# First loads in order of need, and the second feed-forward product by halves of its inner rows

## The chip, the cores and the metric

The kernel runs on one core of a Trainium2 chip. The metric is device microseconds of one execution. The median of three runs of the kernel before is 3042.24 us (3039.03 to 3044.84). The profiled execution, from which the tables below are taken, spans 3047.2 us.

## The reference

Two graph layers are applied to x (64 graphs, 256 nodes, 256 features), with an adjacency matrix of small integers for each graph; all is float32.

```python
# layer 0: two graph attentions, then a feed-forward
def gat(h, W, a):
    Wh = h @ W
    e = leaky_relu(Wh @ a[:256] + (Wh @ a[256:]).T, 0.2)
    att = softmax(where(adj > 0, e, -9e15), axis=1)
    return att @ Wh
h = layernorm(x + gat(gat(x, W1, a1), W2, a2))
x = layernorm(h + relu(h @ w_ff1 + b_ff1) @ w_ff2 + b_ff2)
# layer 1: attention with 8 heads, values by kind of edge, then a feed-forward
s = softmax(q @ k.T / sqrt(32))
o = sum over r in 0..3 of (s * (adj == r)) @ (x @ Wv[r])
x = layernorm(x + o @ Wo + bo)
x = layernorm(x + gelu(x @ W1 + b1) @ W2 + b2)
```

The inner width of both feed-forwards is 1024.

## The kernel before, in words

**Pairs of graphs.** The 64 graphs are handled as 32 pairs, each of which goes the whole way (`whole_way`, L943): the two graph attentions (`gat_layers`, L515), the first feed-forward (`feed_forward` with stage 0), the attention with heads (`attention`, L724), the second feed-forward (stage 2), and the store. Up to four pairs are under way at once. Since the adjacency takes only the values 0 and 1, two kinds of edge are enough; checks of the inputs' range are gathered on the way, and another program (`any_inputs`) would run if they failed.

**An order written out by a planner.** Each way is a Python generator. A step of it that needs TensorE yields the events it waits for, the names of locks it takes (such as "ff"), the number of PSUM banks that it needs, and, in further places, the buffers it needs. Work for the other engines is put into lists with `put` (L158), with a price in us, a rank, what it frees and what it needs. `run` (L213) is a list scheduler: it keeps a clock for each engine, starting at the values in `START` (L29), takes what can begin first, and emits the instructions in that order; `keep_order` then fixes this order on each engine. Loads that are emitted ahead of the planner have an assumed time of arrival: `landed` (L878) for groups of weights and the number given to `load` (L280) for the first two pairs. The planner only assumes them: at run time an instruction waits for its own data, and everything behind it in its engine's queue waits too. Among TensorE steps that could begin at once, the planner prefers those that are neither part of `reliefs` (the one-off preparation of biases) nor hold the lock "ff", so that feed-forwards fill what others leave.

**First loads.** SyncE issues them in the order of the program: the weights for W1 and W2 of layer 0, then the first pair's xT (transposed features), adjT (transposed adjacency) and x; the layernorm vectors; the feed-forward weights; the second pair's three; and then the weights of layer 1. The second pair's xT goes into the one buffer "input", which the first pair's xT holds until its last product of L528. VectorE adds bias vectors together at L899 once they are there, and L901 forms differences of weights.

**Feed-forward.** The first product (256 to 1024) is done with seven block products in place of eight (`Blocks`, L372): p1 to p7 with additions between them. There are two such sets, `slabs(0)` and `slabs(2)`, called a and b, of four of the eight inner blocks of 128 rows each: a has the inner blocks 0, 1, 4, 5 and b has 2, 3, 6, 7. Their results are held in four tiles named ff, two for each set. A chain runs through each set: a product in PSUM is copied by ScalarE (L687), VectorE adds further products to it (L392), and ScalarE applies bias and function (L693). The second product (1024 to 256, L712) has 32 matmuls: for graph b, for half j of its rows, over all eight inner blocks. It uses one PSUM bank for each graph b, and after the last matmul of a graph its layernorm begins. The last step of set b, `b.p3`, is put behind the first four matmuls. The lock "ff" is held from the first block product to the end of the second product.

**Transposing.** Between stages, features are transposed by VectorE in blocks and then by a round trip through DRAM; in five places at the start and the end of the kernel (`hurried`, L604) TensorE does it instead (L649), since then there is little other work to hide the round trip.

**Lines.** L528, L544, L557: the three products of a pair's graph attentions. L464: TensorE spreads a row of factors (first two pairs). L499 and L501: the attention weights on VectorE. L509: their scaling on ScalarE. L303 and L307: the adjacency made into bytes on ScalarE, and its largest values on VectorE. L681: block products of the first product of a feed-forward. L712: second product. L754, L759: queries, keys and values. L796: scores. L825, L828: attention times values, and sums. L847: output projection. L570: addition of the residual. L582 to L598: layernorm. L912, L921: one-off bias products. In the changed kernel these lines stand 6 to 12 further down.

Of the kernel before, what the change touches and what calls it, by code (L numbers as in the profile page):

```python
# [18 lines left out]
P = 128  # L19
# [8 lines left out]
SLACK = 0.3  # L28
START = {"tensor": 8.5, "vector": 8.0, "scalar": 4.0, "gpsimd": 0.0, "sync": 32.0}  # L29


@with_exitstack
def two_layers(ctx: ExitStack, tc: tile.TileContext, t: dict, out: bass.AP, flag: bass.AP):
# [95 lines left out]
    for m in range(KC):  # L129
# [11 lines left out]
    alone = {}  # L141
    free = {name: [0.0] * n for name, n in (("bank", 8), ("a", 2 * HQ), ("m", 2 * HQ), ("h", 2 * HQ), ("yb", 1), ("yT", 2), ("yTa", 1),
                                             ("input", 1), ("rows", 1), ("e", 2), ("adj", 4), ("sums_yT", 1), ("sums_yTa", 1), ("x", 4))}
# [69 lines left out]
    def run(besides, ways, together):  # L213
# [5 lines left out]
        while True:  # L219
# [8 lines left out]
            for n, (way, events, name, banks, *more) in enumerate(going):  # L228
                if all(alone.get(n) in (None, way) for n in name or ()) and all(e.time is not None for e in events):
                    at = begins(max([e.time for e in events], default=0.0), "bank" if banks else None, banks)  # L230
                    for needs in more:
                        at = None if at is None else begins(at, needs)
                    if at is not None:
                        times.append((at, n))
# [8 lines left out]
            if engine == "tensor":  # L243
                sure = [n for at, n in times if at <= now - SLACK]
                g = going[min(sure, key=lambda n: (going[n][0] is besides, "ff" in (going[n][2] or ()) or alone.get("ff") is going[n][0], n))
                          if sure else min(times)[1]]
                alone.update((name, g[0]) for name in g[2] or ())
                takes("bank", g[3])
                for needs in g[4:]:
                    takes(needs)  # L250
                step = next(g[0], None)
# [26 lines left out]


    def load(pair, at=None):  # L280

# [11 lines left out]
        def xT():  # L293
            to["xT"] = io.tile([P, KC, 512], F32, name="input")
            nc.sync.dma_start(to["xT"], t["xT"][pair].rearrange("(c p) b n -> p c (b n)", p=P))
# [24 lines left out]
        takes("x")  # L320
        for emit in (xT, adjT, x):
            emit()
        return to, [at_time(at), in_bytes(at_time(at)), at_time(at)]

# [47 lines left out]
    class Blocks:  # L372
# [24 lines left out]
        def p1(self):  # L397
            yield *self.first, 1
            self.begin()
            self.u1 = self.copy(0, 0, self.product(1, "x", 0, True))  # L400
# [114 lines left out]
    def gat_layers(pair, to, loads):  # L515
# [8 lines left out]
        for b in range(2):  # L524
# [6 lines left out]
            if b == 0:  # L531
                yield [], None, 2
        frees_at(clock["tensor"], ["input"] * (pair > 0))
        at_home, ratio, there = yield from addends(y, there, D + 2, 0, pair)
# [123 lines left out]
    def feed_forward(y, normal, w, func, relieved, gb, pair, stage):  # L658
# [11 lines left out]
        def slabs(t):  # L670
# [25 lines left out]

            first = ([normal[0], normal[1], relieved, second.there[0]], ["ff"]) if t == 0 else ([], None)
            blocks = Blocks(second, first, begin, multiply, target, copy, lambda of, event: activate(1, 0, event, of), activate)
# [3 lines left out]
        for step in (a.p1, b.p1, a.p2, a.p6, b.p2, b.p6, a.p5, a.p7, b.p7, b.p5, a.p4, b.p4, a.p3):  # L702
            yield from step()
        order, end = (0, 1, 4, 5, 2, 3, 6, 7), b.p3
        for b in range(2):
            for j in range(2):
                for part in (order[:half], order[half:]):
                    yield [evacuated[j][m] for m in part] if b == 0 else [], None, j == 0 and part[0] == 0
                    if j == 0 and part[0] == 0:
                        p2 = bank()  # L710
                    for m in part:
                        nc.tensor.matmul(p2[:, j * D:(j + 1) * D], lhsT=f[m][:, (2 * j + b) * P:(2 * j + b + 1) * P],  # L712
                                         rhs=w2[:, m, :], start=m == 0, stop=m == NF - 1)
# [686 lines left out]
```

## Time and profile before

| | |
|---|---|
| median of three runs | 3042.24 us |
| span of the profiled execution | 3047.2 us |
| TensorE matmuls (PE) | 2996.3 us busy, 19146 instructions |
| weight loads (PEld) | 2452.5 us busy |
| VectorE (DVE) | 2556.8 us busy |
| ScalarE (ACT) | 1752.5 us busy |
| GpSimd (POOL) | 252.6 us busy |
| second products of the two feed-forwards (L712) | 470.9 and 456.1 us busy |
| ScalarE loads of function tables | 70, of 1.28 us |
| transfers | 205.76 MB, mean 68 GB/s |

A float32 matmul appears as two instructions. Matmuls overlap, so the mean of one (about 380 ns) is longer than the pace at which they follow each other: eight instructions of L712 take 1.73 us. Busy time of an engine therefore says only when it has something to do. The places where TensorE has nothing to do are found in the idle time before its instructions, with the instruction whose end released it.

### The profile page before, as it was taken

The page shows a single profiled execution, that of the slowest core. Times are in us where ns is not written, and L with a number is a line of the kernel's source. Part 1 is how long each engine was busy: PE and PEld are TensorE (multiplying, and loading weights), DVE is VectorE, ACT ScalarE, POOL GpSimd, SP SyncE. Part 2 cuts the span into 40 slices and gives each one's busy share as a digit, 9 for nine tenths or more (in the row PEclk, how much of TensorE's full clock was granted, in tenths as well). Part 3 has the DMA queues.
Part 4 walks back from the last instruction along what each step waited for, and adds up shares of the span by engine and source line. Part 5 has one row for each costly group of instructions (what it writes and reads, how often), then busy time and mean ns, then how long its engine had stood idle before and what let it go on. Part 6 is the DMA issues. An engine that isn't in the chain of part 4 may idle for free.

```text
span 3047.2 us, 52870 instructions
## 1 busy us (share of the span) xinstructions
PE 2996.3 (98%) x19146; PEld 2452.5 (80%) x19146; DVE 2556.8 (84%) x5993; ACT 1752.5 (58%) x4096; POOL 252.6 (8%) x518
## 2 busy tenths in 40 slices
PE   7999999999999999999999999999999999999998
PEld 6887788878888888888888888888888888788876
DVE  5888988788988888888889888889888898888875
ACT  4556666556556556555565565565555655555654
POOL 0100010001100001100001000011000011000100
PEclk8999999999999999999999999999999999999999
DMA  5211041212212222112222112221122221122100
GB/s 186 74 47 61 32 127 54 70 56 84 70 40 66 77 84 77 53 53 70 84 84 77 39 60 77 84 77 62 50 68 79 84 77 52 52 71 70 49 1 22
DMA packets 211147, 205.76 MB, mean 68 GB/s; under 512 B 22336, under 2 KB 170432, under 8 KB 210880
## 3 DMA queue, kind: packets, MB, share of 16 engines
q1 hardware_dynamic: 210464, 202.06, 20.6%
q8 instruction: 153, 2.51, 0.4%
q14 instruction: 114, 0.93, 0.1%
q10 hardware_dynamic: 416, 0.26, 0.0%
HBM read 137.51 MB, written 64.73 MB: 66 GB/s over the span
## 4 chain that ended last, share of the span: by engine, by line
PE 63%; DVE 25%; DMA 6%; ACT 2%; SPq 1%; issue 1%; POOL 0%; DVEq 0%; ACTq 0%; POOLq 0%
PE ps L712 21%; PE ps L681 15%; PE ps L825 5%; DVE x L598 4%; PE ps L759 4%; PE ps L754 4%; PE ps L544 3%; DVE h L837 3%; PE ps L796 3%; DMA home<-yb 3%; DVE st L582 2%; DVE m L807 2%; PE ps L557 2%; DMA rows<-row 2%; DVE ff L392 2%; PE ps L847 2%
## 5 line engine op out<-in xcount | busy, mean ns | idle before, releaser
L712 PE MATMUL ps<-w_L_gnn_w_ff,ff 128*128 128x256 f32 x2048 | 470.9, 381 | 0.0
L712 PE MATMUL ps<-w_L_gnn_W,ff 128*128 128x256 f32 x2048 | 456.1, 380 | 1.8 <-ACT ff L693 1.8
L593 ACT ACTIVATE x<-x,less,rstd 128x256 f32<-128x256 f32 x512 | 279.2, 596 | 294.8 <-POOL less L589 294.7
L712 PEld LDWEIGHTS ps<-w_L_gnn_w_ff,ff 128*128 128x128 f32 x2048 | 386.6, 190 | 61.5 <-issue 9.8
L712 PEld LDWEIGHTS ps<-w_L_gnn_W,ff 128*128 128x128 f32 x2048 | 388.2, 190 | 57.6 <-ACT ff L693 2.6
L588 POOL TENSOR_TENSOR rstd<-rstd,mhalf 128x2 f32<-128x2 f32 x256 | 198.3, 775 | 2765.7 <-DVE less L585 2638.0
L807 DVE TENSOR_TENSOR m<-a,adj 128x512 f32<-128x512 f32 x512 | 350.1, 684 | 57.9 <-ACT a L803 57.8
L803 ACT ACTIVATE a<-ps 128x512 f32<-128x512 f32 x512 | 268.0, 604 | 222.6 <-PE ps L796 222.5
L681 PE MATMUL ps<-yT,w_L_gnn_W1p 128*128 128x256 f32 x1280 | 315.2, 382 | 4.7 <-ACT ff L687 2.4
L392 DVE TENSOR_TENSOR ff<-ps,ff 128x512 f32<-128x512 f32 x384 | 262.7, 685 | 66.4 <-PE ps L681 58.3
L681 PE MATMUL ps<-yT,w_L_gnn_w_ff1p 128*128 128x256 f32 x1280 | 308.8, 382 | 6.8 <-ACT ff L687 5.9
L681 PEld LDWEIGHTS ps<-yT,w_L_gnn_w_ff1p 128*128 128x128 f32 x1280 | 240.6, 190 | 50.8 <-ACT ff L687 18.8
L687 ACT ACTIVATE ff<-ps 128x512 f32<-128x512 f32 x384 | 223.9, 590 | 98.4 <-PE ps L681 97.6
L681 PEld LDWEIGHTS ps<-yT,w_L_gnn_W1p 128*128 128x128 f32 x1280 | 240.2, 190 | 48.2 <-ACT ps L835 8.5
L837 DVE RECIPROCAL h<-ps 128x256 f32<-128x256 f32 x128 | 223.4, 1746 | 21.3 <-PE ps L828 20.9
L509 ACT ACTIVATE xw<-xw,rs 128x258 f32<-128x258 f32 (+1 forms) x256 | 115.9, 502 | 200.7 <-DVE rs L504 200.6
L693 ACT ACTIVATE ff<-ff,c_L_gnn_b_ff 128x256 f32<-128x256 f32 x384 | 171.6, 504 | 97.4 <-DVE ff L392 97.0
L693 ACT ACTIVATE ff<-ff,c_L_gnn_b 128x256 f32<-128x256 f32 x384 | 173.3, 501 | 85.0 <-DVE ff L392 83.8
L811 DVE TENSOR_TENSOR h<-a 128x256 f32<-128x256 f32 x512 | 213.9, 418 | 0.0
L582 DVE BATCH_NORM_STATS2 st<-x 128x6 f32<-128x256 f32 x512 | 206.0, 402 | 0.9
L570 DVE TENSOR_TENSOR x<-ps,x 128x512 f32<-128x512 f32 x256 | 170.2, 682 | 16.4 <-PE ps L712 9.3
L769 ACT ACTIVATE qk<-ps,bqk 128x256 f32<-128x256 f32 x256 | 106.6, 468 | 112.2 <-PE ps L754 111.9
(128 smaller groups left out, 5008.1 us busy)
## 6 DMA issues: line engine op xcount, KB each, us to landing
home<-yb SPq DMA_DIRECT2D x182, 256.0 KB, 2.0
yT<-home SPq DMA_DIRECT2D x728, 64.0 KB, 2.0
rows<-row SPq DMA_DIRECT2D x60, 512.0 KB, 4.0
input<-in_xT SPq DMA_DIRECT2D x32, 512.0 KB, 5.1
x<-in_x SPq DMA_DIRECT2D x32, 512.0 KB, 3.8
out<-x SPq DMA_DIRECT2D x32, 512.0 KB, 5.1
input<-in_adjT SPq DMA_DIRECT2D x30, 512.0 KB, 4.5
v<-in_adjT SPq DMA_DIRECT2D x2, 512.0 KB, 7.3
```

The lines of the kernel that those rows point to most:

```text
L392: nc.vector.tensor_tensor(self.target(c, h), self.bank[bank], self.target(c, h), ALU.add)
L582: nc.vector.bn_stats(st[:, j, :], rows[j])
L588: nc.gpsimd.tensor_tensor(rstd, rstd, mhalf[:, :2], ALU.pow)
L593: nc.scalar.activation(rows[j], rows[j], AF.Identity, bias=less[:, j:j + 1], scale=rstd[:, j:j + 1])
L681: nc.tensor.matmul(to, lhsT=w1[:, a, (t + slab) * P:(t + slab + 1) * P], rhs=b, **flags)
L687: return put("scalar", 0.5, lambda: nc.scalar.activation(target(c, h), blocks.bank["x"], AF.Copy), event, rank=-1)
L693: evacuated[h][m] = put("scalar", 0.4, lambda m=m, to=to, source=source: nc.scalar.activation(to, source, func, bias=b1[:, m:m + 1]), even ...
L712: nc.tensor.matmul(p2[:, j * D:(j + 1) * D], lhsT=f[m][:, (2 * j + b) * P:(2 * j + b + 1) * P], rhs=w2[:, m, :], start=m == 0, stop=m == N ...
L803: nc.scalar.activation(a[n][o], ps[o], AF.Exp)
L807: nc.vector.tensor_tensor(m[n][o], a[n][o], adj, ALU.mult)
L811: nc.vector.tensor_tensor(h[n][o], a[n][o][:, :N], a[n][o][:, N:], ALU.add)
L837: there = put("vector", 1.68, lambda: nc.vector.reciprocal(s, po[:, N:]), there, rank=0)
```

## The change

The first part changes the order of the first loads: the second pair's xT and adjT are issued ahead of the feed-forward weights, x of each pair later than before, and the second pair's xT goes into the tile qk, which is not in use at that time, so that its load needn't wait for the first pair's. The times that the planner assumes for arrivals and for the engines' starts are set anew.

The second part splits the second product of a feed-forward by its inner rows: first all that the rows of set a contribute, for both graphs and both halves; then all of set b. Both graphs' PSUM banks are thus held throughout. After the first half the two ff tiles of set a are free. The lock "ff" is released when the second product has begun; a new lock "second" covers the rest of it. A first product now asks for two free ff tiles for each set. So the first product of another feed-forward can begin beside the second half of this one. A bank's start flag is set only by its first matmul. Steps that hold "second" have the same low preference as those with "ff".

```diff
-START = {"tensor": 8.5, "vector": 8.0, "scalar": 4.0, "gpsimd": 0.0, "sync": 32.0}
+START = {"tensor": 11.5, "vector": 11.5, "scalar": 4.0, "gpsimd": 0.0, "sync": 36.0}
...
-                g = going[min(sure, key=lambda n: (going[n][0] is besides, "ff" in (going[n][2] or ()) or alone.get("ff") is going[n][0], n))
+                g = going[min(sure, key=lambda n: (going[n][0] is besides, going[n][2] in (["ff"], ["second"]) or going[n][0] in (alone.get("ff"), alone.get("second")), n))
...
         def xT():
-            to["xT"] = io.tile([P, KC, 512], F32, name="input")
+            if at is not None and pair == 1:
+                to["xT"] = work.tile([P, 2, KC, 512], F32, name="qk")[:, 0]
+            else:
+                to["xT"] = io.tile([P, KC, 512], F32, name="input")
...
-        for emit in (xT, adjT, x):
+        for emit in (xT, adjT):
             emit()
-        return to, [at_time(at), in_bytes(at_time(at)), at_time(at)]
+        rest.append(x)
+        return to, [at_time(at[0]), in_bytes(at_time(at[1])), at_time(at[2])]
...
-            first = ([normal[0], normal[1], relieved, second.there[0]], ["ff"]) if t == 0 else ([], None)
+            first = ([normal[0], normal[1], relieved, second.there[0]], ["ff"], ("ff", 2)) if t == 0 else ([], None, ("ff", 2))
...
-        order, end = (0, 1, 4, 5, 2, 3, 6, 7), b.p3
-        for b in range(2):
-            for j in range(2):
-                for part in (order[:half], order[half:]):
-                    yield [evacuated[j][m] for m in part] if b == 0 else [], None, j == 0 and part[0] == 0
-                    if j == 0 and part[0] == 0:
-                        p2 = bank()
+        end, p2 = b.p3, {}
+        for first, part in ((True, (0, 1, 4, 5)), (False, (2, 3, 6, 7))):
+            for b in range(2):
+                for j in range(2):
+                    yield ([evacuated[j][m] for m in part] if b == 0 else []), ["second"] if first and b == j == 0 else None, first and j == 0
+                    if first and j == 0:
+                        p2[b] = bank()
                     for m in part:
-                        nc.tensor.matmul(p2[:, j * D:(j + 1) * D], lhsT=f[m][:, (2 * j + b) * P:(2 * j + b + 1) * P],
-                                         rhs=w2[:, m, :], start=m == 0, stop=m == NF - 1)
+                        nc.tensor.matmul(p2[b][:, j * D:(j + 1) * D], lhsT=f[m][:, (2 * j + b) * P:(2 * j + b + 1) * P],
+                                         rhs=w2[:, m, :], start=first and j == 0 and m == 0, stop=not first and m == NF - 1,
+                                         skip_group_check=True)
                     there = took(0.43 * len(part))
-                    if b == j == 0 and part[0] == 0:
+                    if first and b == 0 and j == 0:
                         yield from end()
                         frees_at(clock["tensor"], ["yT", "sums_yT"])
-            normal[b] = layernorm(y, gb, b, add_rows(y, p2, b, there), *([biased[1]] if onwards else []))
-            if onwards:
-                transposed(y, normal[b], normal, b, pair, 1)
-        done_with("ff")
+                        done_with("ff")
+                if not first:
+                    normal[b] = layernorm(y, gb, b, add_rows(y, p2[b], b, there), *([biased[1]] if onwards else []))
+                    if onwards:
+                        transposed(y, normal[b], normal, b, pair, 1)
+            frees_at(clock["tensor"], ["ff"] * 2)
+        done_with("second")
...
-    landed = {name: at_time(us) for name, us in (("ln0", 8.0), ("ff0", 15.0), ("attention", 30.0), ("ff1", 37.0))}
-    loaded = {0: load(0, 6.5)}
+    landed = {name: at_time(us) for name, us in (("ln0", 13.0), ("ff0", 23.0), ("attention", 35.0), ("ff1", 41.0))}
+    loaded = {0: load(0, (8.0, 9.5, 16.0))}
     ln = [layernorm_weights("L0_gnn_g_ln1", "L0_gnn_b_ln1", "L0_gnn_b_ff2")]
+    loaded[1] = load(1, (14.0, 15.5, 25.0))
+    rest[0]()
     ff0 = (first_weights("L0_gnn_w_ff1p"), column("L0_gnn_b_ff1"), weights("L0_gnn_w_ff2"))
-    loaded[1] = load(1, 18.0)
+    rest[1]()
```

More of the change, by code (lines that the diff above doesn't have):

```diff
@@ L141, in two_layers @@
     alone = {}
-    free = {name: [0.0] * n for name, n in (("bank", 8), ("a", 2 * HQ), ("m", 2 * HQ), ("h", 2 * HQ), ("yb", 1), ("yT", 2), ("yTa", 1),
+    free = {name: [0.0] * n for name, n in (("bank", 8), ("a", 2 * HQ), ("m", 2 * HQ), ("h", 2 * HQ), ("yb", 1), ("ff", NF // 2), ("yT", 2), ("yTa", 1),
                                              ("input", 1), ("rows", 1), ("e", 2), ("adj", 4), ("sums_yT", 1), ("sums_yTa", 1), ("x", 4))}
@@ L231, in run @@
                     for needs in more:
-                        at = None if at is None else begins(at, needs)
+                        at = None if at is None else begins(at, *(needs if isinstance(needs, tuple) else (needs,)))
                     if at is not None:
@@ L249, in run @@
                 for needs in g[4:]:
-                    takes(needs)
+                    takes(*(needs if isinstance(needs, tuple) else (needs,)))
                 step = next(g[0], None)
@@ L277, in of_graph @@
         return slice(2 * b, 2 * b + 2)
+    rest = []
     def load(pair, at=None):
@@ L397, in p1 @@
         def p1(self):
-            yield *self.first, 1
+            yield *self.first[:2], 1, *self.first[2:]
             self.begin()
@@ L532, in gat_layers @@
                 yield [], None, 2
-        frees_at(clock["tensor"], ["input"] * (pair > 0))
+        frees_at(clock["tensor"], ["input"] * (pair != 1))
         at_home, ratio, there = yield from addends(y, there, D + 2, 0, pair)
```

## The prediction

> **What bounds the kernel now.** I read the shares of busy time first, then TensorE's busy time in stretches of 100 us, then what TensorE waited for, and last the first 52 us and the end, instruction by instruction.
>
> The page's first part (busy us, share of the span, instructions):
>
> ```profile
> span 3047.2 us, 52870 instructions
> PE 2996.3 (98%) x19146; PEld 2452.5 (80%) x19146; DVE 2556.8 (84%) x5993; ACT 1752.5 (58%) x4096; POOL 252.6 (8%) x518
> ```
>
> TensorE is idle for 50.9 us in all. The change alters no matmul in shape or number (the order of instructions of both programs counts equally many of each shape). So nothing but those 50.9 us, and TensorE's slow clock at the start, can be won. Where they lie, from the stretches of 100 us (start:end, length, then busy us of PE, PEld, DVE, ACT, POOL, the granted clock, DMA):
>
> ```profile
> 0.00:100.00 100.00, 78.80 (x489) 67.25 (x490) 59.82 (x184) 48.98 (x124) 5.16 (x14) 0.90 0.51 159
> 300.00:400.00 100.00, 96.72 (x737) 73.37 (x732) 95.08 (x215) 63.17 (x150) 4.42 (x10) 1.00 0.14 48
> 1500.00:1600.00 100.00, 100.00 (x633) 82.17 (x631) 84.50 (x196) 56.91 (x133) 7.83 (x16) 1.00 0.21 69
> 2900.00:3000.00 100.00, 96.96 (x825) 74.64 (x818) 78.58 (x163) 58.33 (x133) 5.83 (x13) 1.00 0.02 7
> 3000.00:3047.20 47.20, 34.15 (x211) 28.57 (x209) 21.23 (x52) 16.61 (x34) 4.93 (x10) 0.91 0.08 24
> ```
>
> Idle: 21.2 us in the first 100, about 13.7 between 100 and 2900, 3.0 between 2900 and 3000, and 13.0 after that, of which 11.5 follow the last matmul. What TensorE waited for, longest first (total us, times, longest):
>
> ```profile
> PE ps L557 <- ACT xw L509: 9.3, 1, 9.3
> PE ps L681 <- ACT ff L687: 9.1, 18, 1.4
> PE ps L127 <- DMA a<-in_L_gnn_W1T: 7.5, 1, 7.5
> PE ps L544 <- ACT xw L509: 4.5, 2, 3.5
> ```
>
> The third is the first bytes arriving and stays. The first is the largest. Behind it stands VectorE, which serves its queue in order and sits before a bias load (start us, us, then the idle before it and who ended that):
>
> ```profile
> 39.65 0.43 DVE L899 TENSOR_TENSOR b_L_gnn_beta<-b_L_gnn_beta,ff 128x256 f32<-128x256 f32 x1 [4.84 <-DMA b_L_gnn_beta<-in_L_gnn_beta]
> 40.33 0.48 DVE L499 SCALAR_TENSOR_TENSOR e<-rows,ratio 128x256 f32<-128x256 f32 x1
> 43.98 6.11 PE L557 MATMUL ps<-xw,e 128*128 128x256 f32 x16 [9.26 <-ACT xw L509]
> ```
>
> Pair 0's second attention weights (L499) are queued behind that addition. The second line of waits, at most 1.4 us a time, is the chain of seven block products in a first feed-forward product, waiting for a ScalarE copy. It is all that the overlap of feed-forwards could remove.
>
> **What the Trainium skill says.** "TensorE: Matmul & The Clock Gate", What's actually happening: the array runs at half clock after an idle window of about 3.4 us, until it has been busy about as long. The trace agrees: clock 0.50 from 40 to 48 us, where the 16 matmuls of L557 need 5.95 us to the next instruction, against 3.45 at the pace of later ones (8 of L712 in 1.73 us). The same page, Architectural detail, calls VectorE and ScalarE strict FIFO; the L899 stall above is that. "ScalarE: Activation LUTs", What ACT_TABLE_LOAD costs: 1283 ns and a drain of 1380 ns. The trace has 70 loads of 1283 ns, but work goes on 1.30 us after one begins (load at 1254.97, next activation 1256.27); I use 1.3. "PSUM — Partial Sum Buffer", The four PSUM rules: a start flag clears a whole bank's bits, later matmuls without it overwrite where bits are clear. This covers starting a bank only at its first matmul; it costs no time.
>
> **Part by part.**
>
> *First loads.* The second pair's xT goes into an unused tile. Before, SyncE waited 3.1 us for L528 to release the buffer, and loads behind it slipped. I moved the issues on, keeping the old rule that no more than eight loads are out at once: the key weights' issue goes from 25.1 to about 22.6 us, and the beta load's from 33.4 to between 29.6 and 30.9. It landed 6.1 us after issue (33.42 to 39.55); with the same, 35.7 to 37.0. In the new order of instructions the beta addition still stands ahead of pair 0's second weights. So the wait stays, 2.5 to 3.8 us earlier, and the first half of L557 can begin at 40.0 to 41.4 instead of 43.98.
>
> But ScalarE's order now has pair 2's adjacency conversion (L303 before) between the two halves' scalings. That load landed 8.3 us after issue, at 48.6; issued 2.5 to 3.8 us earlier, behind the same megabytes, it lands at 44.8 to 46.1. Then conversion 1.06 and two scalings 0.91: the second half begins at 46.8 to 48.1 and takes 1.7 to 3.5 us by clock. TensorE goes on to the bias products at 48.5 to 51.5, where it was 50.8. Further on, the new order leaves only the eight transposes of L464 (0.9 us) between the last transposing of pair 0 and its first block product. Before, 1.75 us of L528 stood there too. ScalarE's row copies (the last 0.4), the transposed copy 0.55 and VectorE's sums 0.42 come before that product, some 1.4 us idle. Start in sum: between 4 us won and 2 lost; I take 0. Other edits of load order move work that nothing waits for (weights that landed before use).
>
> *Second product by halves.* 32 matmuls stay 32, so 13.8 us a feed-forward stay. p2 holds two banks for the whole product, instead of one for half of it. The order shows 10 more changes from a full-array matmul to the scores (98 to 108, and 30 to 20 from the attention products), at some 0.1 us each (scores begin at 1224.85, where eight of L712 from 1223.03 would end at 1224.76): 1 us. Both graphs' layernorms now come 3.5 us apart instead of 6.9; VectorE is 84% busy, and other pairs' matmuls hide it, except at the end.
>
> *Next first product beside it.* The most it wins is the 13.7 us of the middle. Whether it does is open: in the new order the first product runs bare for 24 or 26 matmuls in 30 of 64 feed-forwards, against 4 of 64, so its own copies have less cover; but query and key products are now filled in with second products, which need no ScalarE copy. Gelu and exp also alternate oftener: table loads 70 to 110, 40 x 1.3 = 52 us on an engine with over 1200 us free. Bounds: nothing if all lie in ScalarE's idle time, 52 if none do. Chain steps have 0.9 to 1.7 us of slack, so a load overhangs by some 0.2 on average where it falls in a chain, in perhaps half of the cases: 4 us. I set this against 4 won by fewer copy conflicts. Middle: 0, from -10 to +15.
>
> *The end.* This is on the path. In the old order the last pair's output projection (two groups of 4 matmuls) is followed, before the last feed-forward, by 4 + 8 + 8 second products of the pair before (8.6 us); they hide the last layernorms. In the new one, 4 remain (1.7 us), the other 16 having been done earlier. The chain is not shorter: add 0.7, statistics 1.3, root 1.3, normalising 1.1, scaling 1.4 for each graph, VectorE interleaving both. In the old trace (each matmul is two instructions):
>
> ```profile
> 2996.46 1.89 PE L847 MATMUL ps<-w_L_gnn_Wo,qk 128*128 128x256 f32 x8
> 2998.18 3.62 PE L712 MATMUL ps<-w_L_gnn_W,ff 128*128 128x256 f32 x16
> 3001.78 1.08 PE L649 MATMUL ps<-ident,x 128*32 128x128 f32 x32
> 3002.79 3.72 PE L712 MATMUL ps<-w_L_gnn_W,ff 128*128 128x256 f32 x16
> 3007.20 1.08 PE L649 MATMUL ps<-ident,x 128*32 128x128 f32 x32 [0.69 <-DVE x L598]
> 3008.99 2.86 PE L681 MATMUL ps<-yT,w_L_gnn_W1p 128*128 128x256 f32 x12 [0.71 <-ACT yT L653]
> ```
>
> The two L712 lines of 16 instructions (1.73 us for 8, so 6.9 for both) are what the new order lacks here. Without them the first block product (L681) still begins some 10.7 us after the projection's end at 2998.3: TensorE stands idle that much longer, over 3.4 us at a stretch, so the feed-forward starts at half clock and loses another 0 to 1.7. End: +6 to +9; I take +8. The 11.5 us after the last matmul stay, since 3.5 us still separate the two last graphs' statistics.
>
> Sum: 3042.2 + 0 + 0 + 8 = 3050.
>
> **The rivals.**
> - Faster: the middle loses most of its waits (-10), the start wins its 4, and half of the end's 8 is repaid by less idle time shortly before: 3042 - 14 + 4 = 3032. For it: the copy waits repeat, and the overlap is new freedom. Against: most stretches are at 99.5% and over.
> - No change: the middle and the start win 5 to 8, the end takes it: 3042.
> - Much slower: table loads fall into the chains, a third of 52 us shows, plus the end: 3042 + 17 + 8 = 3067. Against: 58% busy ScalarE.
>
> **How the numbers follow.** The forecast 0.47, no change 0.20, faster 0.18, much slower 0.15. The bound of 0.2% is 6 us: below 3036 only the faster case; between 3036 and 3048 the no-change case and a fifth of the forecast's; the rest slower. Range: 3034 to 3063.
>
> **What would show it.** The first matmuls of L557 (in the changed kernel L563) at 40 to 41.4 us, split by a wait for the conversion; 110 table loads; between 100 and 2900 about as much idle as now; two waits of TensorE for x and yT near the end, 5 us and more in all, with a clock under 1. It is wrong if the end is filled after all, if the middle's copy waits vanish, or if the adjacency lands by 42 us.

## The result, and the profile after

The changed kernel takes 3131.74 us (median; 3128.93 to 3133.19), the kernel before, on the same chip, 3041.38 us (3039.03 to 3044.84). The ratio is 1.0292, 95% interval 1.0277 to 1.0308: 90 us slower, where 8 us slower was forecast.

The page's first part for the changed kernel (busy us, share of the span, instructions):

```profile
span 3131.4 us, 52943 instructions
PE 3032.5 (97%) x19146; PEld 2462.1 (79%) x19146; DVE 2571.5 (82%) x5993; ACT 1816.9 (58%) x4136; POOL 270.2 (9%) x518
```

TensorE has the same 19146 instructions, and is idle for 98.9 us instead of 50.9. ScalarE has 40 instructions more, all of them loads of function tables. Its share of busy time is 58%, as before. The stretches of the changed kernel, with the columns of the prediction (PE, PEld, DVE, ACT, POOL, clock, DMA share, GB/s):

```profile
0.00:100.00 100.00, 79.05 (x428) 66.76 (x428) 57.57 (x178) 45.79 (x117) 5.33 (x14) 0.88 0.47 149
300.00:400.00 100.00, 93.58 (x652) 74.14 (x654) 88.10 (x207) 61.63 (x137) 8.27 (x16) 0.98 0.20 65
1400.00:1500.00 100.00, 96.60 (x692) 75.45 (x685) 89.33 (x196) 63.98 (x151) 8.39 (x14) 0.99 0.17 54
3000.00:3131.40 131.40, 111.70 (x830) 87.99 (x828) 85.60 (x190) 64.09 (x135) 10.77 (x20) 0.92 0.04 14
```

The middle is where the time went. Summed over the 28 stretches from 100 to 2900 us, TensorE's idle time rises from 13.6 to 58.3 us, and the clock below 1 costs 10 us (100 us times what is missing to 1, added up) where it cost nothing. In the same 2800 us it does 17126 instructions instead of 17629; 503 fewer, at 0.159 us each on average, is some 80 us of work. The first 100 us and the time after 2900 account for about 2 and 10 us (idle time and clock together). Some 18 us of the 84 between the two profiled spans are neither idle time nor lower clock by this sum.

What TensorE waited for between 100 and 2900 us (total us, times, longest), before:

```profile
PE ps L681 <- ACT ff L687: 7.4, 15, 1.4
PE ps L754 <- ACT qk L769: 1.3, 3, 0.8
```

and after (L687 here is L681 before; L693 is the copy, L699 bias and function, L813 the exponential of the scores, L848 the scaled output of the heads):

```profile
PE ps L687 <- ACT ff L693: 15.0, 26, 1.4
PE ps L857 <- DVE qk L848: 14.8, 6, 2.5
PE ps L718 <- ACT ff L699: 13.3, 15, 2.8
PE ps L687 <- DVE sums_yT L365: 3.7, 1, 3.7
```

The copy waits, which the overlap could have removed, doubled. Two waits came new: the second product for its gelu (L699), and the output projection for VectorE (L848). The table loads, by the function that needed them (times, total us, ns of one), before:

```profile
L693 ACT ACT_TABLE_LOAD x35 | 44.9, 1283 | 0.6
L803 ACT ACT_TABLE_LOAD x8 | 10.3, 1283 | 0.1
```

and after:

```profile
L699 ACT ACT_TABLE_LOAD x55 | 70.6, 1283 | 0.9
L813 ACT ACT_TABLE_LOAD x41 | 52.6, 1283 | 0.7
```

Before, ScalarE switched from gelu to the scores' exponential 8 times; after, 41 times. (The remaining loads stand at the exponentials of the graph attentions, 26 before and 13 after, and one at the start.) One pair's gelu now meets another pair's attention. What that does is seen in a stretch that comes back every four pairs (381 us), in order of time (start us, us, engine and line; in brackets the idle time before it and who ended it):

```profile
1480.78 1.28 ACT L813 ACT_TABLE_LOAD   x1
...
1482.69 1.28 ACT L699 ACT_TABLE_LOAD   x1
...
1484.51 1.13 PE L718 MATMUL ps<-w_L_gnn_W,ff 128*128 128x256 f32 x4 [0.57 <-ACT ff L699]
...
1485.56 1.28 ACT L813 ACT_TABLE_LOAD   x1
...
1488.45 1.28 ACT L699 ACT_TABLE_LOAD   x1
...
1489.74 2.51 ACT L699 ACTIVATE ff<-ff,c_L_gnn_b 128x256 f32<-128x256 f32 x6
...
1492.15 2.06 ACT L599 ACTIVATE x<-x,less,rstd 128x256 f32<-128x256 f32 x4
...
1493.26 0.69 DVE L604 TENSOR_TENSOR x<-x,b_L_gnn_g_ln 128x512 f32<-128x512 f32 x1 [2.28 <-ACT x L599]
...
1494.60 3.36 DVE L847 RECIPROCAL h<-ps 128x256 f32<-128x256 f32 x2
1497.88 0.69 DVE L848 TENSOR_TENSOR qk<-ps,h 128x256 f32<-128x256 f32 x2
...
1498.29 3.58 PE L857 MATMUL ps<-w_L_gnn_Wo,qk 128*128 128x256 f32 x8 [2.46 <-DVE qk L848]
```

Read it upwards from the last line. TensorE waits for L848. That stands behind two reciprocals, which stand behind L604 in VectorE's queue. L604 waits for a layernorm's normalising (L599) on ScalarE. And L599 comes late since ScalarE has worked without a pause from 1480.8: four table loads, 5.1 us, in 9 us. The page calls this a wait for VectorE; its source is ScalarE. Then L857 takes 3.42 us to the next product (at 1501.71), where eight instructions at full clock take 1.73.

At the start of the changed kernel three things are to be seen. First, SyncE's two waits before the load of the second pair's adjacency (ns of the shortest, middle and longest; first and last start); the longer, 4.26 us from 9.8, ends at 14.06. Then VectorE's addition of the beta vector, and the two halves of L563:

```profile
L293 SPq EVENT_SEMAPHORE  x2: 17/2138/4260, 7.6 to 9.8; - x2
```

```profile
42.99 0.43 DVE L911 TENSOR_TENSOR b_L_gnn_beta<-b_L_gnn_beta,ff 128x256 f32<-128x256 f32 x1 [3.88 <-DMA b_L_gnn_beta<-in_L_gnn_beta]
```

```profile
47.33 3.73 PE L563 MATMUL ps<-xw,e 128*128 128x256 f32 x8 [8.30 <-ACT xw L515]
...
53.39 1.99 PE L563 MATMUL ps<-xw,e 128*128 128x256 f32 x8 [1.46 <-ACT xw L515]
```

Beta came 3.3 us later than before (39.65), not earlier. And the end of the changed kernel:

```profile
3075.74 1.89 PE L718 MATMUL ps<-w_L_gnn_W,ff 128*128 128x256 f32 x8
3077.47 1.97 PE L857 MATMUL ps<-w_L_gnn_Wo,qk 128*128 128x256 f32 x8
3085.27 1.94 PE L655 MATMUL ps<-ident,x 128*32 128x128 f32 x32 [5.84 <-DVE x L604]
3088.51 1.94 PE L655 MATMUL ps<-ident,x 128*32 128x128 f32 x32 [1.30 <-DVE x L604]
3091.15 5.02 PE L687 MATMUL ps<-yT,w_L_gnn_W1p 128*128 128x256 f32 x12 [0.71 <-ACT yT L659]
```

The transposes wait 5.84 and 1.30 us for layernorms that second products used to hide, and the first block products then run at half clock (4.86 us for 12 instructions to the next product, 2.6 at full clock).

### The profile page after: what moved, and what is told of

The parts are those of the page before. It is cut to its first block, busy times and chain, and to the rows that moved or that the text cites. A ratio compares the mean times of both kernels' runs of the same rounds, so it can differ in the third digit from the quotient of the medians.

```text
span 3131.4 us, 52943 instructions
## 1 busy us (share of the span) xinstructions
PE 3032.5 (97%) x19146; PEld 2462.1 (79%) x19146; DVE 2571.5 (82%) x5993; ACT 1816.9 (58%) x4136; POOL 270.2 (9%) x518
## 4 chain that ended last, share of the span: by engine, by line
PE 69%; DVE 16%; ACT 8%; DMA 4%; issue 1%; SPq 1%; POOL 0%; DVEq 0%; ACTq 0%; POOLq 0%
PE ps L718 22%; PE ps L687 16%; PE ps L764 6%; PE ps L769 6%; PE ps L835 5%; PE ps L806 4%; ACT ff L699 3%; PE ps L563 3%; DVE x L604 3%; PE ps L550 3%; DVE h L847 3%; PE ps L534 2%; DVE st L588 2%; PE ps L857 2%; DVE x L576 2%; DMA home<-yb 1%
## 5 line engine op out<-in xcount | busy, mean ns | idle before, releaser
L599 ACT ACTIVATE x<-x,less,rstd 128x256 f32<-128x256 f32 x512 | 277.9, 593 | 361.1 <-POOL less L595 361.1
L718 PE MATMUL ps<-w_L_gnn_W,ff 128*128 128x256 f32 x2048 | 470.5, 383 | 13.1 <-ACT ff L699 10.3
L813 ACT ACTIVATE a<-ps 128x512 f32<-128x512 f32 x512 | 269.7, 601 | 155.7 <-PE ps L806 154.9
L687 PE MATMUL ps<-yT,w_L_gnn_W1p 128*128 128x256 f32 x1280 | 316.2, 385 | 4.6 <-ACT ff L693 3.4
L687 PE MATMUL ps<-yT,w_L_gnn_w_ff1p 128*128 128x256 f32 x1280 | 308.7, 382 | 7.9 <-ACT ff L693 5.3
L693 ACT ACTIVATE ff<-ps 128x512 f32<-128x512 f32 x384 | 222.1, 590 | 108.0 <-PE ps L687 106.1
L687 PEld LDWEIGHTS ps<-yT,w_L_gnn_W1p 128*128 128x128 f32 x1280 | 241.2, 191 | 51.5 <-ACT ff L693 13.3
L687 PEld LDWEIGHTS ps<-yT,w_L_gnn_w_ff1p 128*128 128x128 f32 x1280 | 240.1, 190 | 51.4 <-ACT ff L693 9.3
L515 ACT ACTIVATE xw<-xw,rs 128x258 f32<-128x258 f32 (+1 forms) x256 | 116.1, 503 | 197.0 <-DVE rs L510 196.8
L699 ACT ACTIVATE ff<-ff,c_L_gnn_b_ff 128x256 f32<-128x256 f32 x384 | 174.9, 502 | 58.8 <-DVE ff L398 58.0
L699 ACT ACTIVATE ff<-ff,c_L_gnn_b 128x256 f32<-128x256 f32 x384 | 173.4, 501 | 24.6 <-DVE ff L398 23.5
```

Of the source, the lines that this page charges most:

```text
L599: nc.scalar.activation(rows[j], rows[j], AF.Identity, bias=less[:, j:j + 1], scale=rstd[:, j:j + 1])
L687: nc.tensor.matmul(to, lhsT=w1[:, a, (t + slab) * P:(t + slab + 1) * P], rhs=b, **flags)
L693: return put("scalar", 0.5, lambda: nc.scalar.activation(target(c, h), blocks.bank["x"], AF.Copy), event, rank=-1)
L699: evacuated[h][m] = put("scalar", 0.4, lambda m=m, to=to, source=source: nc.scalar.activation(to, source, func, bias=b1[:, m:m + 1]), even ...
L718: nc.tensor.matmul(p2[b][:, j * D:(j + 1) * D], lhsT=f[m][:, (2 * j + b) * P:(2 * j + b + 1) * P], rhs=w2[:, m, :], start=first and j == 0 ...
L813: nc.scalar.activation(a[n][o], ps[o], AF.Exp)
```

## The experiments

My theory after the result: the overlap brings gelu and the scores' exponential into the same stretches, so that ScalarE, with table loads, becomes the bound there. Rivals: the split itself costs (less cover for the last copies of set b); the new first loads do it; or it is one unlucky course of the planner, which small edits change throughout. All ratios below are to the kernel before on the same chip. Differences between two runs are differences of their medians; where these come from different chips, some 3 us of a difference can be the chip's, since the kernel before takes 3041.2 to 3044.9 us on the chips used.

**Which part.** The first loads alone (the old feed-forward and preference in the changed kernel), the second part alone (the new ones with the old loads), and the changed kernel with the lock "ff" held to the end, so that nothing overlaps:

```diff
                         frees_at(clock["tensor"], ["yT", "sums_yT"])
-                        done_with("ff")
...
         done_with("second")
+        done_with("ff")
```

- loads_only. 

> The first part of the change alone (order of first loads, times that the planner assumes); the second product and its lock as before. 72 table loads stand in its program, as before. Theory T (gelu of one pair's feed-forward now alternates with exp of another's attention, and ScalarE loses its time to table loads): 3036 to 3048 us, about the time before. Rival S (the new assumed times shift the whole plan): over 3080 us. Either way the wait for the beta load stands.

  Measured 3048.45 us, 1.0014 (1.0008 to 1.0021).
- no_overlap. 

> The changed kernel with the lock ff held to the end of the second product, so that it is still split by inner rows, but no other first product begins beside it; 72 table loads stand in its program. Theory T: 3036 to 3056 us. Rival R (the split itself, with two banks held, layernorms 3.5 us apart and less slack for the results of the first product): over 3090 us, near the changed kernel.

  Measured 3081.59 us, 1.0123 (1.0106 to 1.0140).
- ff_only. 

> The split and the overlap with the first loads of the kernel before (110 table loads as in the changed kernel). If the parts add up, the changed kernel less what the loads alone cost: 3131.7 - 4.5, so 3120 to 3133. If the order of loads and the split need each other (a shifted start throws the plan of the middle), it falls outside, below 3115 or above 3140.

  Measured 3114.31 us, 1.0228 (1.0211 to 1.0246).

So of 90 us, the loads took 4.5, the split without overlap 33 (3048.5 to 3081.6), the overlap 50 (3081.6 to 3131.7). With the old loads the second part alone costs 70, where 86 would be left of the 90: the shares depend on the plan in which they are taken. The split's share I had not expected; no_overlap lies between what my theory and its rival said.

The rival's explanation seemed to fit one place of no_overlap. At 273.03 the second product waits 2.59 us for the gelu of the other half's rows (j = 1) of set a, which the split asks for at once after the last block product; in the old order the rest of the first half (1.7 us) came in between:

```profile
267.80 1.28 ACT L813 ACT_TABLE_LOAD   x1
...
271.18 1.28 ACT L699 ACT_TABLE_LOAD   x1
...
273.03 2.71 PE L718 MATMUL ps<-w_L_gnn_W,ff 128*128 128x256 f32 x8 [2.59 <-ACT ff L699]
```

But two table loads stand before that gelu on ScalarE, and with relu in its place (no_overlap_relu, below) the second product follows at 270.12 without any wait. So this wait belongs to the table loads, and the split's own cost has to be looked for elsewhere.

**Table loads.** The same programs with relu in place of gelu, with the planner still counting a table for it, so that order and prices stay. They compute another function in layer 1 and serve only to measure the loads: one load is left in each, and one relu takes ScalarE as long as one gelu (504 and 501 ns in the changed kernel):

```diff
-        kind = "gelu" if func == AF.Gelu else None
+        kind = "gelu" if stage == 2 else None
...
-... ff1, AF.Gelu, relieved[2], ln[3], pair, 2)
+... ff1, AF.Relu, relieved[2], ln[3], pair, 2)
```

- after_relu. 

> The changed kernel in the same order on every engine, but the second feed-forward's gelu is replaced by relu, which needs no other table than exp; so another function is computed in layer 1, and all table loads but the first are gone. Theory T: 3045 to 3070 us (the unfilled end and the start stay). Rivals R and O (two overlapping chains of copies and additions, whatever the tables): over 3105 us.

  Measured 3096.25 us, 1.0176 (1.0159 to 1.0193).
- before_relu. 

> The same replacement of gelu by relu in the kernel before, as a control: 70 table loads gone there, in the same order. Theory T: 3025 to 3041 us, since its table loads lie in ScalarE's idle time; if it falls by as much as the changed kernel does with relu, table loads do not explain the difference.

  Measured 3039.21 us, 0.9982 (0.9975 to 0.9989).
- no_overlap_relu. 

> The kernel that splits the second product but keeps the lock to its end, with gelu replaced by relu in layer 1 (another function is computed there; no table loads but the first), in the same order. If table loads hurt only beside the overlap (theory T as the runs so far leave it), it is 3 to 8 us below the split kernel with gelu, as in the kernel before: 3073 to 3079 us. If the split's cost too is table loads: under 3055 us.

  Measured 3070.87 us, 1.0089 (1.0071 to 1.0107).

Without table loads the kernels differ by 31.7 (split and loads) and 25.4 us (overlap). With them, the loads cost 4.7 us in the kernel before, 10.7 with the split, 35.5 with the overlap. So of the overlap's 50 us, about 25 are table loads. In the changed kernel's order without them, TensorE's idle time between 100 and 2900 us falls from 58.3 to 32.6 us, and the waits named above fall too: the projection's for VectorE from 14.8 to 1.1 us (the longest from 2.5 to 0.2), and the two for ScalarE, 15.0 and 13.3 us, to

```profile
PE ps L687 <- ACT ff L693: 8.4, 11, 1.4
PE ps L718 <- ACT ff L699: 7.7, 9, 1.3
```

That confirms the reading of the stretch at 1480. after_relu lies between what my theory and its rivals said, and each holds in part. Of the overlap's other 25 us, some 7 are the unfilled end, which no_overlap does not have (the wait of L655 for x is 7.1 us in after_relu). The rest is open: TensorE's whole idle time is nearly the same in after_relu and no_overlap_relu (72.7 and 68.9 us), but it is busy 16 us longer with the same instructions.

Where the 31.7 us come from is seen in TensorE's waits for the copies of the first product, in before_relu and then in no_overlap_relu:

```profile
PE ps L681 <- ACT ff L687: 4.0, 10, 0.7
```

```profile
PE ps L687 <- ACT ff L693: 25.1, 25, 2.4
```

These 21 us are two thirds of the 31.7. In 21 of the 25 waits (23.4 us), as in 19 of the 25 of no_overlap and in 18 of the 22 of no_overlap_slack5 (below), the same chain stands before the copy, about once a pair, in the feed-forward of layer 0. In no_overlap:

```profile
1506.02 0.48 DVE L505 SCALAR_TENSOR_TENSOR e<-rows,ratio 128x256 f32<-128x256 f32 x1 [2.89 <-DMA rows<-row]
...
1508.79 0.91 ACT L515 ACTIVATE xw<-xw,rs 128x258 f32<-128x258 f32 x2 [2.31 <-DVE rs L510]
...
1509.61 0.89 ACT L699 ACTIVATE ff<-ff,c_L_gnn_b_ff 128x256 f32<-128x256 f32 x2
...
1510.40 1.05 ACT L693 ACTIVATE ff<-ps 128x512 f32<-128x512 f32 x2
...
1511.03 1.13 PE L687 MATMUL ps<-yT,w_L_gnn_w_ff1p 128*128 128x256 f32 x4 [1.98 <-ACT ff L693]
```

The copy (L693) stands in ScalarE's queue behind the scaling (L515) of another pair's attention weights. That scaling waits for VectorE, which had to wait for these weights' rows to come back from DRAM. VectorE waits for such rows just as long in before_relu (44.7 us, against 46.2 in no_overlap_relu); there the copies hardly wait. So most of the split's cost seems to come from what its plan puts in front of the copies. No run takes this chain away, so its share is read from the traces alone; why the plan changes in this place is not settled.

Two checks on whether it is the number of loads. In after_table, ScalarE's list takes work of the table in place first; in before_slack15, another SLACK (how long a step must have been ready to be chosen by preference) gives the kernel before nearly as many loads as the changed one (102), but no overlap.

```diff
-... min(able, key=lambda n: (waiting[engine][n]["rank"], waiting[engine][n]["ready"])))
+... min(able, key=lambda n: (waiting[engine][n]["function"] not in (None, table[0]), waiting[engine][n]["rank"], waiting[engine][n]["ready"])))
...
-SLACK = 0.3
+SLACK = 0.15
```

- after_table. 

> The changed kernel with one more rule: ScalarE takes work that needs no other table first, whatever its rank. 90 table loads stand in its program in place of 112. Theory T (each table load beside the overlap costs nearly 1 us): 20 loads fewer give 15 to 25 us less than the changed kernel, 3105 to 3118 us. If it is the overlap as such, or the split, it stays over 3120 us, or rises since urgent copies now wait longer.

  Measured 3119.14 us, 1.0253 (1.0236 to 1.0270): 22 loads fewer, 12.6 us less. The rule changes the whole plan, so not all of this need be the loads.
- before_slack15. 

> The kernel before with the planner's tolerance SLACK at 0.15 us in place of 0.3: no split and no overlap, but an order with 104 table loads in place of 72. Theory T, table loads cost whatever the order around them: 3065 to 3085 us. If loads cost only because gelu of one pair and exp of another then share a stretch in which ScalarE is full, or if they are harmless: under 3055 us.

  Measured 3067.79 us, 1.0079 (1.0062 to 1.0096).

The second lies in the range that I had given for table loads which cost the same everywhere. But its longest waits do not point to its loads:

```profile
PE ps L681 <- DMA yT<-home: 12.9, 8, 2.7
...
PE ps L649 <- DVE x L598: 7.1, 2, 5.8
...
PE ps L681 <- ACT ff L687: 6.4, 13, 1.5
```

It waits for transposes through DRAM and for an unfilled end; the waits for ScalarE's copies are no longer than in the kernel before (9.1). Before two of the waits for DRAM (those ending at 915.43 and 1481.53) ScalarE had been idle for 8 us, so no table load stands behind them. It was not run with relu, so what its loads cost is not measured; that a hundred loads do little harm where gelu and the exponential are not crowded into one stretch is likely, not shown.

**The change, or one course of the plan.** SLACK 0.5 plans everything anew. These four are the kernel before, the split without overlap, the changed kernel, and that with relu.

- before_slack5. 

> The kernel before with SLACK at 0.5 us: 80 table loads. It shows how far any other order from the same planner lies from the one chosen. Theory T: 3045 to 3060 us. If the orders before and after differ mainly by luck of the planner, this lies 20 us and more above the time before.

  Measured 3053.40 us, 1.0036 (1.0022 to 1.0050).
- no_overlap_slack5. 

> The split without overlap, planned with SLACK at 0.5 us. With that value the unsplit kernel took 3053 us, of which 8 are an unfilled end; its middle ran without a wait, 92.0 us a pair. If the split costs cover in itself (the results of the second half of the rows are asked for 1.7 us earlier): still 25 us and more over that, 3078 to 3090 us, with TensorE waiting for ScalarE before second products. If the steady loss of the split was luck of the planner: 3055 to 3068 us.

  Measured 3076.20 us, 1.0106 (1.0089 to 1.0123).
- after_slack5. 

> The changed kernel planned with SLACK 0.5 in place of 0.3, another course of the plan throughout, with 102 table loads. The split without overlap cost 3076 in such a plan. If the cost of the overlap is inherent (gelu of one pair beside exp of another on a full ScalarE), 3105 to 3140. If it was this one plan's bad luck, 3065 to 3095.

  Measured 3120.25 us, 1.0246 (1.0229 to 1.0263).
- after_slack5_relu. 

> The same with relu in place of gelu in layer 1 (another function is computed; the plan is kept, and next to no table loads remain). If table loads cost the more where the overlap is, as in the plan with SLACK 0.3 (35 us), 25 to 40 us less than the run with gelu. If they hurt only in that plan, 0 to 15 us less.

  Measured 3099.50 us, 1.0184 (1.0167 to 1.0201).

In this plan split and loads cost 23 us and the overlap 44 more; 21 us go with the table loads, fewer than the 25 to 40 that I expected. The sizes shift, the order stays. For the overlap that speaks against the bad luck of one plan; the split's 23 us are no more than another SLACK alone costs the kernel before (before_slack15: 26), but the same chain stands before its waits in both plans. Where TensorE waits in after_slack5 between 100 and 2900 us:

```profile
PE ps L718 <- ACT ff L699: 23.6, 17, 2.9
PE ps L687 <- ACT ff L693: 11.7, 25, 0.7
```

Here the second product's wait for gelu leads, and the projection's wait for VectorE is gone. What waits changes with the plan; in both plans the longest new waits are for ScalarE, directly or, as at 1480, by way of VectorE.

**Giving the split its cover back.** after_j takes the first half as graph 0 and graph 1 of half j = 0, then of j = 1:

```diff
-            for b in range(2):
-                for j in range(2):
+            for b, j in ((0, 0), (1, 0), (0, 1), (1, 1)) if first else ((0, 0), (0, 1), (1, 0), (1, 1)):
...
-                if not first:
+                if not first and j == 1:
```

- after_j. 

> The changed kernel with the first half of the second product in another order: both graphs for the first half of the rows, then both for the second half, so that 4 more matmuls (1.7 us) stand between the last block product and what needs its result. Its program has 88 table loads in place of 112. If lost cover before second products is a large part of the change's cost, TensorE's waits there (15.7 us) mostly vanish, and with 24 loads fewer the time is 3090 to 3112 us. If not, over 3120.

  Measured 3254.24 us, 1.0689 (1.0671 to 1.0707).

That failed. Its longest waits of the middle:

```profile
PE ps L857 <- DVE qk L848: 23.2, 7, 3.8
PE ps L687 <- ACT ff L693: 19.9, 25, 1.6
```

The wait of the second product for gelu has left the top of the list, as meant, but the planner took a wholly different course, and other waits replaced it. So this run does not tell what the lost cover is worth.

**The start.** late_before tells the planner of the kernel before that the weights of layer 1 land at 60 us, so that VectorE isn't held by the beta addition. loads_v and after_v are the first part alone and the changed kernel with both first adjacencies in one tile v, its two halves, instead of asking for the buffer twice (`shared` makes the tile at the first call).

```diff
-landed = {... ("attention", 30.0), ("ff1", 37.0))}
+landed = {... ("attention", 60.0), ("ff1", 60.0))}
...
-                to["adjT"] = work.tile([P, 2, 2, 2 * D], F32, name="v")[:, pair].bitcast(I32).rearrange(
+                to["adjT"] = shared()[:, pair].bitcast(I32).rearrange(
```

- late_before. 

> The kernel before, with the planner told that layer 1's weights arrive at 60 us (it had 30 and 37). The addition that waits for the beta load then stands behind the attention weights of pairs 0 and 1 on VectorE, and the conversion of pair 2's adjacency behind both scalings on ScalarE. If the prediction's account of the start holds, the first L557 begins at 39 to 40 us instead of 44 and is not split, and the time falls by 3 to 9 us, to about 3037; if another wait takes its place, it stays within 2 us of the time before.

  Measured 3054.63 us, 1.0045 (1.0028 to 1.0062). The first wait shrank as said, but the bias products that had filled the next gap went elsewhere, and a longer wait took its place. I had put that case within 2 us of the time before; it is 13 us slower, of which the idle time of the first 100 us explains 3.7 (24.9 instead of 21.2); the rest was not followed. The waits:

```profile
39.88 5.41 PE L557 MATMUL ps<-xw,e 128*128 128x256 f32 x16 [4.26 <-ACT xw L509]
...
57.39 4.97 PE L544 MATMUL ps<-xw,e 128*128 128x258 f32 x14 [11.23 <-ACT xw L509]
```

- loads_v. 

> The first part of the change alone, with both first adjacencies in the two halves of one tile v instead of two uses of one buffer. The planned order of instructions is as in the first part alone (3048.5). If SyncE's wait for the first adjacency's last reader (4.26 us, to 14.06) delays all later first loads, the second adjacency is issued by about 10 us, the addition of the beta vector comes 3 to 4 us earlier than at 42 to 43, and the first L563 (here some lines on) begins at 42 to 44 instead of 46.6: 3043 to 3047. If another limit of the loads stands behind it (eight transfers at once), the issue of beta moves by under 1.5 us and the time stays at 3047 to 3050.

  Measured 3044.21 us, 1.0006 (0.9997 to 1.0015).
- after_v. 

> The changed kernel with that one edit. If the start's wait is the same and nothing else depends on it, 3 to 5 us below the changed kernel: 3126 to 3130. If the loads' limit is another, 3130 to 3133. In no case does it repay a tenth of the 90 us.

  Measured 3124.77 us, 1.0269 (1.0252 to 1.0286).

In loads_v the load is issued at 7.82 us in place of 14.07, and everything behind it moves:

```profile
7.82 0.47 SPq L298 DMA_DIRECT2D v<-in_adjT  x1
```

```profile
39.21 0.42 DVE L912 TENSOR_TENSOR b_L_gnn_beta<-b_L_gnn_beta,ff 128x256 f32<-128x256 f32 x1 [5.40 <-DMA b_L_gnn_beta<-in_L_gnn_beta]
```

So the semaphore wait of 4.26 us delayed the later loads. Its repair wins some 3 to 4 us (loads; the intervals of the two ratios overlap) and 7 us (the whole change, a little more than expected). What is left of the first part is then no gain and no loss that can be measured.

**A version that beats both.** In before_slack5 the middle ran almost without waits from 700 us on (0.6 us of idle time up to 2900), and only what comes earlier and the end lost. mid_slack is the kernel before with SLACK 0.5 from pair 6 to 27 and 0.3 elsewhere; mid_loads_v does the same to loads_v.

```diff
-                sure = [n for at, n in times if at <= now - SLACK]
+                sure = [n for at, n in times if at <= now - slack[0]]
...
+        slack[0] = 0.5 if 6 <= pair < NPAIR - 4 else SLACK
```

- mid_slack. 

> The kernel before, planned with SLACK at 0.5 us between pairs 6 and 27 and at 0.3 before and after; 72 table loads, and its last layernorms have all their 20 second products to hide behind. If the waits of the middle (about 0.6 us a pair over 92.0) vanish as they did with 0.5 throughout, and the end stays filled: 3026 to 3036 us, faster than both kernels. If the pieces do not fit together: 3040 us or more.

  Measured 3037.47 us, 0.9978 (0.9969 to 0.9987).
- mid_loads_v. 

> The first part alone with the shared tile v and with SLACK 0.5 for pairs 6 to 27, which took 4 us off the kernel before. If both gains add up, 3036 to 3041, thus not clearly below the 3037.5 of the kernel before with SLACK 0.5 in the middle. If the middle's gain belongs to the plan that starts with the old loads, 3043 to 3047.

  Measured 3037.17 us, 0.9982 (0.9975 to 0.9989).

Both beat the kernel before, by some 7 and 5 us; the new loads add nothing. The one wait of the middle that was left has shrunk; over the whole of mid_slack it is 4.1 us (9.1 before):

```profile
PE ps L681 <- ACT ff L687: 4.1, 9, 0.7
```

## Why the prediction was wrong

The direction was right, the size was not. Two terms of the sum carry most of the error: the table loads, by some 27 us, and the split, by a similar amount; for some 18 us of the overlap no cause is shown.

- *"Next first product beside it ... Middle: 0, from -10 to +15."* This failed. The term of the table loads ("some 0.2 on average where it falls in a chain, in perhaps half of the cases: 4 us") measured 31 us more than in the kernel before (35.5 against 4.7). I priced a load against the slack of one chain step and against ScalarE's idle time of the whole run. But the extra loads do not fall anywhere: they fall where gelu and exponentials alternate, which is where ScalarE has most to do, and four of them came in one such stretch. There the delay goes through the layernorm into VectorE's queue. The Trainium skill has a rule for this: "ScalarE: Activation LUTs", Table sets, advises to batch activations by set and not by function; after_table goes that way, with 12.6 us less for 22 loads fewer, though in another plan. The term set against it ("4 won by fewer copy conflicts") had the wrong sign: those waits rose from 7.4 to 15.0 us.
- *"Second product by halves ... 1 us."* Also too small. Split and loads without overlap and without table loads cost 31.7 us, of which the loads alone are 4.5. I counted the matmuls and changes of shape, and put the new plan's effect on ScalarE's queue at nothing. There the copies of the first product now stand behind another pair's scaling that waits for rows from DRAM: 25.1 us of waits instead of 4.0.
- *"Start in sum ... I take 0."* Near in size (about +2 us until 100 us, +4.5 by loads_only), wrong in its working. The beta load was issued at 36.26, not between 29.6 and 30.9, since removing the wait on "input" uncovered one on v, which is asked for again for the second pair and is only freed when VectorE has read the first pair's adjacency (14.0). The limit of eight loads out at once, on which the estimate rested, is seen in the old trace: SyncE has issued six and ScalarE two by 3.72, and the ninth is issued at 6.50, just after one of them has landed (6.45). But it was not what held the loads here. The first half of L563 began at 47.33, not at 40.0 to 41.4. That it splits in two, and the 1.14 us before the first block product, came as said.
- *"End: +6 to +9; I take +8."* Right: 7.1 us of waits for x and the half clock that follows.
- The rival "much slower" had the right mechanism at a third of 52 us; 31 of the 52 showed, and the split came on top. Its counter-argument, "58% busy ScalarE", is the mistake: it is an average over stages with different limits.

What stays open is why the split's plan puts the copies behind that scaling, and the 16 us for which TensorE is busy longer with the overlap. The run that was to give the split its cover back replanned everything and says nothing on either.

## What to carry to other kernels

When a change lets two stages run side by side, ask what both need of the engine that is not the bound, within that stretch of time and in its queue, and not over the whole run; functions from two tables on one engine are the first thing to count. When a step is cut in two, look at what the new order puts ahead of each urgent copy in its engine's queue, and not only at how many instructions the pieces have: here a copy stood behind work that waited for a transfer. When a wait on one buffer is removed from an in-order queue of loads, look for the next reuse of a buffer behind it.

## What the runs showed that was not expected

- A wait of 2.46 us was enough for half clock afterwards (eight instructions of L857 in 3.42 us instead of 1.73; clock 0.50 from 1498.3 to 1501.5). The Trainium skill, "TensorE: Matmul & The Clock Gate", What's actually happening, names an idle window of about 3.4 us; this trace shows the slow clock after a shorter single wait, preceded by short ones. So this wait cost 4.15 us, 1.7 times its length.
- The cost of a table load depends on its place: taking out all loads but one won 4.7 us of 69 loads in the kernel before, and 35.5 us of 109 in the changed kernel. 102 loads (131 us) made no wait for ScalarE's copies longer in one plan without overlap (before_slack15).
- A wait for ScalarE had its source in a transfer several steps back, by way of the queues of VectorE and ScalarE (no_overlap, 1506 to 1511).
- A change of the order within one product moved the whole plan by 120 us (after_j), and a change of SLACK by 0.15 us by 26. A list scheduler's result must be looked at anew after each edit.
